# A mixture-of-experts pass whose first 256 tokens go through all experts as a dense layer, with smaller rooms for the rest and the weights loaded first

## The chip, the core and the metric

The kernel runs on one core of one Trainium2 chip. A core has TensorE (PE, matrix products; its weight loads are shown apart as PEld), VectorE (DVE), ScalarE (ACT), GpSimd (POOL) and SyncE (SP, which here only issues DMAs), and 16 DMA engines which all queues share. The metric is the device time of one execution in microseconds; given is the median of three runs.

## The reference, cut to what matters

The input is 8 sequences of 512 tokens with 128 features. Three residual steps follow each other: half a mixture-of-experts feed-forward, an attention with 16 heads of 8, and the same feed-forward again (same weights).

```python
def _L0_ffn_ref(x, router_w, router_b, W1, b1, W2, b2):     # 8 experts, 2 chosen, 128 -> 512 -> 128
    logits = jnp.einsum('bsd,de->bse', x, router_w) + router_b
    topk_scores, topk_idx = jax.lax.top_k(logits, TOP_K)
    topk_gates = jax.nn.softmax(topk_scores, axis=-1)
    onehot = jax.nn.one_hot(topk_idx, NUM_EXPERTS, dtype=x.dtype)
    combine = jnp.einsum('bsk,bske->bse', topk_gates, onehot)
...
    def expert_step(acc, params):
        w1, bb1, w2, bb2, c = params
        h = jax.nn.relu(jnp.einsum('bsd,df->bsf', x, w1) + bb1)
        y = jnp.einsum('bsf,fd->bsd', h, w2) + bb2
        return (acc + y * c[..., None], None)
...
x = L0_attn_x
x = x + 0.5 * _L0_ffn_ref(_layernorm(x, axis=-1), L0_ffn_router_w, ...)
x = x + _L0_attn_ref(_layernorm(x, axis=-1), L0_attn_w_qkv, L0_attn_w_o, L0_attn_log_xi)
x = x + 0.5 * _L0_ffn_ref(_layernorm(x, axis=-1), L0_ffn_router_w, ...)
```

Each token counts in only two of the eight experts. Everything is float32.

## The kernel before

**Tokens in rooms.** The kernel does not run every token through every expert. It forms six groups of sequences: f0 (sequences 0 and 1), f1 (2 to 4) and f2 (5 to 7) for the first feed-forward, g0, g1 and g2 for the second. `route` normalises a sequence, computes the router's logits on PE, ranks the experts on DVE, and counts with a few products by a triangle of ones (L844 to L852) which place in its expert's room each token gets. Eight indirect DMAs of POOL for each sequence (`scatter`, L875: four tiles of 128 tokens by two choices) then write the normalised rows into a buffer in memory, `xs`. A room is one expert's share of that buffer; for f0 it has 351 rows, for the others 480 (351 again for g0). Since a room is seldom full, `clear` (L700) first fills the buffer with zeros, which SP copies out of a tile of zeros.

**An expert's pass.** `experts` goes through a group's rooms. For each expert it fetches the room (L933), transposes it on PE (L976), ACT copies it out (L980), PE makes the four 128-wide slices of the hidden layer (`wide`, L989; called z), ACT applies bias and relu (L996), PE makes the outputs, one tile of up to 128 rows after the other (`out`, L1013; called y), DVE adds the bias (L1017), and SP writes the rows to a second buffer, `ys` (L1024). Products of one expert stand between those of the next in an order written out in `experts`. A fetch is issued about two experts ahead. `combine` gathers a token's two rows from `ys` by indirect DMAs of POOL (L474) and adds them, weighted, to `x` on DVE (L1073).

**What sets the order.** PE, ACT, DVE and SP keep the order in which the program records their instructions. POOL's transfers are entered in a list (`enter`) and taken from it by `transfer`. The program is a sequence of units, -30 to 125. The units from 0 to 95 each do one piece of attention; in all of them a plan (`plan`) says which group's expert pieces fill the unit: f0 from -30 to -16, f1 from -16 to 7, and so on. `at`, `routed` and `combined` put the routing, gathering and attention's projections at given units. Ahead of unit -30 stands a part that is written out by hand with `step` and `transfers`: the normalising of sequences 0 to 4 and the routing of 0, 1 and part of 2, with their scatters, so that f0 can be fetched.

**What SP loads, and when.** Ahead of the hand-written part SP issues, in this order, x of sequences 0 and 1, the clear of f0's buffer, x of 2, the weights and bias rows of experts 0 to 3 with x of 3 and 4 and the clear of f1's buffer between them, and small constants. The rest (`self.loads`: experts 4 to 7, x of 5 to 7, the attention weights, the clear of f2's buffer) is taken two at a time at the end of each unit from -30. All of SP's DMAs go through one queue, and each waits for the eighth before it.

**Pads.** Attention uses four tiles of 128 x 2048 (query, key, and two for values), which must be zero where no head writes. `slots` has ACT fill them at the start, 1.9 us each (L718). Small constants are written into them by `attention_constants` in unit -30.

**PSUM.** Up to unit 0 one pool of eight banks holds all products (`bank`).

## Time and profile before

| | us |
|---|---|
| median of 3 runs (715.65 to 717.79) | 716.47 |
| the profiled execution | 700.09 |
| its span on the core | 698.3 |
| PE busy | 629.2 (90%) |
| DVE busy | 410.2 (59%) |
| ACT busy | 341.3 (49%) |
| POOL busy | 300.3 (43%) |
| PE busy in the first 40 us of the span | 9.8 |
| f0's first transposes on PE | at 40.71 |
| f1's first transposes on PE | at 91.42 |

Sums and stages are read from the profiled execution, whose own time is 16 us under the median of the runs. Durations in the profile are from an instruction's start to its end; since products on PE overlap, what one of them costs is the distance between starts. In the rows by time, each digit is the busy share of one fortieth of the span (17.5 us) in tenths. Moved bytes: 61.06 MB over the span, 42.51 of them by SP's queue and 17.63 by POOL's indirect DMAs.

### The profile page before, as it was taken

The page shows a single profiled execution, that of the slowest core. Times are in us where ns is not written, and L with a number is a line of the kernel's source. Part 1 is how long each engine was busy: PE and PEld are TensorE (multiplying, and loading weights), DVE is VectorE, ACT ScalarE, POOL GpSimd, SP SyncE. Part 2 cuts the span into 40 slices and gives each one's busy share as a digit, 9 for nine tenths or more (in the row PEclk, how much of TensorE's full clock was granted, in tenths as well). Part 3 has the DMA queues.
Part 4 walks back from the last instruction along what each step waited for, and adds up shares of the span by engine and source line. Part 5 has one row for each costly group of instructions (what it writes and reads, how often), then busy time and mean ns, then how long its engine had stood idle before and what let it go on. Part 6 is the DMA issues. An engine that isn't in the chain of part 4 may idle for free. (4 is left out here: it accounts for less than half of the span.)

```text
span 698.3 us, 13045 instructions
## 1 busy us (share of the span) xinstructions
PE 629.2 (90%) x4867; PEld 410.3 (59%) x4867; DVE 410.2 (59%) x1442; ACT 341.3 (49%) x548; POOL 300.3 (43%) x322
## 2 busy tenths in 40 slices
PE   3269999999999999999999999999999998969980
PEld 2148867756465656556656656656456656747760
DVE  6736448734466666675687677676666654433414
ACT  4034443455755656565665565555665552234420
POOL 3744637642223223314154423424144556575660
PEclk9999999999999999999999999999999999889995
DMA  8747843312409921111211111101402111145324
GB/s 265 197 136 209 205 115 98 85 45 77 101 22 172 264 69 38 30 29 43 71 32 49 40 38 38 30 27 39 105 27 75 35 31 42 53 121 140 104 58 143
DMA packets 78670, 61.06 MB, mean 87 GB/s; under 512 B 7392, under 2 KB 70792, under 8 KB 78600
## 3 DMA queue, kind: packets, MB, share of 16 engines
q1 hardware_dynamic: 69608, 42.51, 23.8%
q0 software_dynamic: 8704, 17.63, 8.5%
q8 instruction: 41, 0.67, 0.4%
q14 instruction: 29, 0.24, 0.1%
q10 hardware_dynamic: 288, 0.01, 0.0%
HBM read 26.34 MB, written 33.78 MB: 86 GB/s over the span
## 5 line engine op out<-in xcount | busy, mean ns | idle before, releaser
L1208 ACT ACTIVATE ee<-st 128x768 f32<-128x768 f32 (+1 forms) x192 | 159.0, 881 | 104.1 <-PE st L1201 100.6
L474 POOL DMA_INDIRECT yt_f<-ys,back_f x64 | 64.8, 1013 | 133.5 <-DVE ee L1215 55.7
L1215 DVE TENSOR_TENSOR ee<-ee,keep 128x256 f32<-128x256 f32 (+1 forms) x192 | 93.5, 507 | 25.4 <-ACT ee L1208 25.3
L1013 PEld LDWEIGHTS y_g<-w_sb,h_g 128*120 128x120 f32 (+1 forms) x704 | 87.1, 184 | 27.4 <-issue 21.7
L875 POOL DMA_INDIRECT xs<-xn_g,to_g x64 | 63.8, 998 | 90.1 <-DVE ee L1215 34.9
L1013 PEld LDWEIGHTS y_f<-w_sb,h_f 128*120 128x120 f32 (+1 forms) x704 | 85.9, 182 | 28.5 <-issue 16.2
L1201 PE MATMUL st<-qT,kT 32*128 32x512 f32 (+3 forms) x1024 | 96.1, 467 | 2.3 <-ACT h_f L996 0.8
L1013 PE MATMUL y_f<-w_sb,h_f 128*120 128x128 f32 (+1 forms) x704 | 93.9, 277 | 0.2 <-DVE h_f L998 0.2
L989 PE MATMUL z_g<-xT_g,w_sb 128*128 128x480 f32 (+1 forms) x192 | 92.6, 569 | 1.3 <-ACT xT_g L980 1.3
L1013 PE MATMUL y_g<-w_sb,h_g 128*120 128x128 f32 (+1 forms) x704 | 93.0, 277 | 0.6 <-DVE o_tok L1250 0.3
L1227 PE MATMUL o<-ee,vpad 128*32 128x512 f32 (+3 forms) x1024 | 89.4, 442 | 0.8 <-DVE ee L1215 0.8
L989 PE MATMUL z_f<-xT_f,w_sb 128*128 128x480 f32 (+1 forms) x192 | 88.8, 551 | 1.0 <-ACT xT_f L980 1.0
L996 ACT ACTIVATE h_f<-z_f,b1T 128x480 f32<-128x480 f32 (+1 forms) x86 | 53.5, 623 | 68.2 <-PE z_f L989 67.3
L957 POOL DMA_INDIRECT ys<-ysb_g,home_g x64 | 63.7, 996 | 39.3 <-ACT h_g L996 8.7
L1017 DVE TENSOR_TENSOR ysb_f<-y_f,b_sb 120x128 f32<-120x128 f32 (+1 forms) x88 | 25.0, 287 | 77.9 <-PE y_f L1013 74.2
L996 ACT ACTIVATE h_g<-z_g,b1T 128x480 f32<-128x480 f32 (+1 forms) x71 | 45.7, 646 | 47.4 <-PE z_g L989 46.7
L1201 PEld LDWEIGHTS st<-qT,kT 32*128 32x128 f32 x1024 | 43.1, 183 | 32.6 <-issue 8.1
L1017 DVE TENSOR_TENSOR ysb_g<-y_g,b_sb 120x128 f32<-120x128 f32 (+1 forms) x88 | 25.1, 287 | 58.2 <-PE y_g L1013 57.6
L1227 PEld LDWEIGHTS o<-ee,vpad 128*32 128x32 f32 x1024 | 23.5, 108 | 52.4 <-issue 7.5
L875 POOL DMA_INDIRECT xs<-xn_n,to_f x40 | 39.0, 974 | 34.9 <-ACT xi_sb L727 8.1
L989 PEld LDWEIGHTS z_g<-xT_g,w_sb 128*128 128x128 f32 x192 | 30.1, 195 | 26.6 <-issue 15.2
L989 PEld LDWEIGHTS z_f<-xT_f,w_sb 128*128 128x128 f32 x192 | 30.2, 194 | 13.8 <-issue 7.2
(186 smaller groups left out, 778.7 us busy)
## 6 DMA issues: line engine op xcount, KB each, us to landing
w_sb<-in_L_ffn_W_dram SPq DMA_DIRECT2D x16, 256.0 KB
xs<-zeros SPq DMA_DIRECT2D x8, 487.5 KB
xb_g<-xs SPq DMA_DIRECT2D x16, 243.8 KB
xb_f<-xs SPq DMA_DIRECT2D x16, 240.0 KB
ys<-ysb_f SPq DMA_DIRECT2D x16, 240.0 KB
ys<-zeros SPq DMA_DIRECT2D x2, 1536.0 KB
x<-in_L_attn_x_dram SPq DMA_DIRECT2D x8, 256.0 KB
xs<-zeros SPq DMA_DIRECT2D x1, 1920.0 KB
```

What stands on the lines that cost most here:

```text
L474: ins = op(*args, **kw)
L875: ins = nc.gpsimd.indirect_dma_start(out=g.xs[:, :], out_offset=bass.IndirectOffsetOnAxis(ap=g.to[:, i, t, r : r + 1], axis=0), in_=xn[:, ...
L957: ins = nc.gpsimd.indirect_dma_start(out=g.ys[:, :], out_offset=bass.IndirectOffsetOnAxis(ap=home[e][:rows, t : t + 1], axis=0), in_=ys[:r ...
L989: nc.tensor.matmul(z[:, :n], self.w1_sb[:, e, ts(c, P)], xT[:, n0 : n0 + n], start=True, stop=True,)
L996: ins = nc.scalar.activation(dst, z[:, :n], AF.Relu, bias=bias)
L1013: nc.tensor.matmul(y[:rows], h[:, c, ts(t, rows)], self.w2_sb[:, e, c, :], start=(c == 0), stop=(c == C - 1),)
L1017: ins = nc.vector.tensor_tensor(ys[:rows, t, :], y[:rows], self.b2_sb[:rows, e], ALU.add)
L1201: nc.tensor.matmul(st[:, h, c0 : c0 + N - kt * P], kT[r0 : r0 + SLOT, ts(kt, P)], qT[r0 : r0 + SLOT, kt * P :], start=True, stop=True,)
L1208: nc.scalar.activation(ee[:, two, :width], st[:, two, :width], AF.Exp)
L1215: ins = self.nc.vector.tensor_tensor(d, d, self.keep.unsqueeze(1).unsqueeze(1).to_broadcast([P, 2, len(parts), P]), ALU.min,)
L1227: self.nc.tensor.matmul(self.o[h * SLOT : (h + 1) * SLOT, kt * P :], self.vpads[b % 2][:, kt, 4 * g + h, :], ee[:, h, c0 : c0 + n], start= ...
```

## The change

It has four parts.

1. **A dense layer.** The first 256 tokens of sequence 0 (`f0.skip[0] = 2`, two tiles of 128) are no longer scattered, fetched and gathered. A new function, `dense`, runs them through all eight experts straight from the transposed rows which the router uses as well, and adds each expert's output to x with the token's gate for that expert (`shares`, zero for the six that were not chosen). Its pieces stand between the steps of the hand-written part.
2. **Smaller rooms.** f0 has 252 rows for each expert, in two tiles of 126, instead of 351 in three of 117; its buffer is cleared in pieces of 1 KB. It has 12 scatters instead of 16, and sequence 0 four gathers instead of eight. g0 keeps 351 rows.
3. **Weights first.** All eight experts' weights are issued ahead of the hand-written part, with the clear of f0's buffer after the first, and x of 2 to 4 and the clear of f1's buffer further back. The bias rows of the second product, spread over the partitions, and the attention constants are loaded from the list from unit -30 on. The column biases (`bias_columns`) are prepared at the very start.
4. **Blanks by DMA.** The four pads are filled by SP's queue from the tile of zeros (`blank`), in the same list, instead of by ACT. `attention_constants` moves from unit -30 to -14.

The core of the diff:

```diff
-ROOMS = [(2, 351, False), (3, 480, False), (3, 480, False), (3, 480, True), (3, 480, True)]
+ROOMS = [(2, 252, False), (3, 480, False), (3, 480, False), (3, 480, True), (3, 480, True)]
...
-        self.clear(0)
-        self.load_x(2)
         self.w1_sb = const.tile([P, E, FF], FP, name="w1_sb")
         self.w2_sb = const.tile([P, E, C, D], FP, name="w2_sb")
         self.b2_sb = const.tile([P, E, D], FP, name="b2_sb")
+        b1_sb = load("b1_sb", [E * C, P], aps["b1"].rearrange("e (c p) -> (e c) p", p=P), nc.scalar)
+        self.b2_rows = load("b2_rows", [E, D], aps["b2"], nc.scalar)
+        for e in range(E):
+            self.load_expert(e)
+            if e == 0:
+                self.clear(0)
+            if e == 3:
+                self.load_x(2)
+        self.load_x(3, 4)
+        self.clear(1)
         self.slots()
-        b1_sb = load("b1_sb", [E * C, P], aps["b1"].rearrange("e (c p) -> (e c) p", p=P))
-        for e in range(4):
-            self.load_expert(e, True)
-            self.load_expert(e, False)
-            if e == 0:
-                self.load_x(3, 4)
-            if e == 2:
-                self.clear(1)
-        self.rope_sb = load("rope_sb", [P, 2, T, DH], aps["rope"])
-        pos_sb = load("pos_sb", [P, T], aps["pos"])
-        xi_sb = load("xi_sb", [P, H], aps["log_xi"].partition_broadcast(P))
+        self.rope_sb = const.tile([P, 2, T, DH], FP, name="rope_sb")
+        pos_sb = const.tile([P, T], FP, name="pos_sb")
+        xi_sb = const.tile([P, H], FP, name="xi_sb")
         self.wqkv_sb = const.tile([P, 3 * D], FP, name="wqkv_sb")
         self.wo_sb = const.tile([P, D], FP, name="wo_sb")
-        self.loads = deque(partial(self.load_expert, e, up) for e in range(4, E) for up in (True, False))
-        self.loads.insert(3, partial(self.load_x, 5))
-        self.loads.insert(6, partial(self.load_x, 6))
+        self.loads = deque(
+            partial(nc.sync.dma_start, dst, src) for dst, src in (
+                *((self.b2_sb[:, e], aps["b2"][e].partition_broadcast(P)) for e in range(E)),
+                (self.rope_sb, aps["rope"]), (pos_sb, aps["pos"]),
+                (xi_sb, aps["log_xi"].partition_broadcast(P)),
+            )
+        )
+        self.loads.append(partial(self.load_x, 5))
+        self.loads.extend(partial(self.blank, pad) for pad in (self.qpad, self.kpad, *self.vpads))
         self.loads.extend([
-            partial(nc.sync.dma_start, self.wqkv_sb, aps["w_qkv"]), partial(self.load_x, 7),
-            partial(nc.sync.dma_start, self.wo_sb, aps["w_o"]),
+            partial(self.load_x, 6), partial(nc.sync.dma_start, self.wqkv_sb, aps["w_qkv"]),
+            partial(self.load_x, 7), partial(nc.sync.dma_start, self.wo_sb, aps["w_o"]),
         ])
         self.loads.extend(partial(self.clear, 2, t) for t in range(4))
...
-    def load_expert(self, e, up):
+    def load_expert(self, e):
         nc, aps = self.nc, self.aps
-        if up:
-            nc.sync.dma_start(self.w1_sb[:, e, :], aps["w1"][e])
-        else:
-            nc.sync.dma_start(self.w2_sb[:, e], aps["w2"][e].rearrange("(c p) d -> p c d", p=P))
-            nc.sync.dma_start(self.b2_sb[:, e], aps["b2"][e].partition_broadcast(P))
+        nc.sync.dma_start(self.w1_sb[:, e, :], aps["w1"][e])
+        nc.sync.dma_start(self.w2_sb[:, e], aps["w2"][e].rearrange("(c p) d -> p c d", p=P))
+
+    def blank(self, pad):
+
+        flat = pad.rearrange("p t h s -> p (t h s)")
+        self.nc.sync.dma_start(
+            flat.rearrange("p (a d) -> p a d", d=T * D),
+            self.zeros[:, : T * D].unsqueeze(1).to_broadcast([P, flat.shape[1] // (T * D), T * D]),
+        )
 
...
-        for t_ in (self.qpad, self.kpad, *self.vpads):
-            self.nc.scalar.copy(
-                t_.rearrange("p t h s -> p (t h s)"),
-                self.zeros[:, 0:1].to_broadcast([P, T * H * SLOT]),
-            )
-
...
+        if g.skip[i]:
+            self.dense_xT = xnT
...
         pp = self.bank([P, 512], f"pos_ps_{key}")
         pos = pp[:, : T * E].rearrange("p (t e) -> p t e", e=E)
-        nc.tensor.matmul(pos, self.earlier, mask, start=True, stop=False)
-        for t in range(T - 1):
+        nc.tensor.matmul(pos[:, t0:], self.earlier, mask[:, t0:], start=True, stop=False)
+        for t in range(t0, T - 1):
             nc.tensor.matmul(
...
-        self.enter([partial(scatter, t, r) for t in range(T) for r in range(2)], urgent, ahead)
+        self.enter(
+            [partial(scatter, t, r) for t in range(t0, T) for r in range(2)], urgent, ahead
+        )
...
+        if t0:
+            shares = small.tile([P, t0, E], FP, tag="shares", name=f"shares_{key}")
+            nc.vector.scalar_tensor_tensor(
+                shares, rank[:, :t0], 2.0, ex[:, :t0], ALU.is_lt, ALU.mult
+            )
...
+        if t0:
+            nc.vector.tensor_tensor(
+                shares, shares, g.gates[:, i, :t0, 0:1].to_broadcast([P, t0, E]), ALU.mult
+            )
+            self.shares = shares
...
+    def dense(self, b, nt):
+
+        nc = self.nc
+        n = nt * P
+        x = self.x[b]
+        h = {}
+
+        def up(e):
+            h[e] = self.fp.tile([P, C, CAP], FP, tag="h", name=f"h_d_{e}")
+            for k in range(0, C, 2):
+                z = self.bank([P, 2, n], f"z_d_{e}_{k}")
+                for j in range(2):
+                    nc.tensor.matmul(
+                        z[:, j], self.w1_sb[:, e, ts(k + j, P)], self.dense_xT[:, :n],
+                        start=True, stop=True,
+                    )
+                for j in range(2):
+                    c = k + j
+                    nc.scalar.activation(
+                        h[e][:, c, :n], z[:, j], AF.Relu, bias=self.b1T[:, e * C + c : e * C + c + 1]
+                    )
+
+        def down(e):
+            y = self.bank([P, nt, D], f"y_d_{e}")
+            for t in range(nt):
+                for c in range(C):
+                    nc.tensor.matmul(
+                        y[:, t], h[e][:, c, ts(t, P)], self.w2_sb[:, e, c, :],
+                        start=(c == 0), stop=(c == C - 1),
+                    )
+
+            def add():
+                for t in range(nt):
+                    nc.vector.scalar_tensor_tensor(
+                        x[:, t, :], y[:, t], self.shares[:, t, e : e + 1], x[:, t, :],
+                        ALU.mult, ALU.add,
+                    )
+
+            return add
+
+        up(0)
+        yield
+        adds = []
+        for e in range(E):
+            if e + 1 < E:
+                up(e + 1)
+                yield
+            adds.append(down(e))
+            while len(adds) > 2:
+                adds.pop(0)()
+            yield
+        for add in adds:
+            add()
+
+        tp = self.bank([P, 512], "shT_ps")
+        for t in range(nt):
+            nc.tensor.transpose(tp[:E, ts(t, P)], self.shares[:, t, :], self.ident)
+        sT = self.const.tile([E, n], FP, name="shT")
+        nc.scalar.copy(sT, tp[:E, :n])
+        yield
+        bp = self.bank([P, nt, D], "b2_ps")
+        for t in range(nt):
+            nc.tensor.matmul(bp[:, t], sT[:, ts(t, P)], self.b2_rows, start=True, stop=True)
+        nc.vector.tensor_tensor(x[:, :nt], bp, x[:, :nt], ALU.add)
+        yield
...
-        self.enter([partial(gather, t, r) for t in range(T) for r in range(2)], urgent, ahead)
+        self.enter(
+            [partial(gather, t, r) for t in range(g.skip[i], T) for r in range(2)], urgent, ahead
+        )
...
-        f0 = m.open_group([0, 1], 351, 0, "f0")
+        f0 = m.open_group([0, 1], 252, 0, "f0")
+        f0.skip[0] = 2
...
-            r = [m.route(f0, 0, early=True), m.route(f0, 1, early=True), m.route(f1, 0, True, early=True)]
+            r = [
+                m.route(f0, 0, early=True), m.route(f0, 1, early=True),
+                m.route(f1, 0, True, early=True),
+            ]
+            d = m.dense(0, f0.skip[0])
+            m.bias_columns()
             step(n[0], n[0], n[1], n[1], n[0], n[0])
-            step(r[0], n[1], n[1], r[0], r[1], r[0], r[0])
+            step(r[0], n[1], n[1], r[0], d, r[1], r[0], d, r[0])
+            transfers(4)
+            step(d, r[0], r[1], d, r[0], r[1], d, r[0], r[1], n[2], n[2])
             transfers(8)
-            step(r[1], r[1], r[1], n[2], n[2])
+            step(d, d, n[2], n[2], d, r[2], d, r[1], d, r[2], d, r[1], d, r[2], r[1], d)
+            step(n[3], n[3], n[4], n[4], r[2], d)
             transfers(8)
-            step(n[3], n[3], n[4], n[4], *[r[0], r[1]] * 3, n[2], n[2])
-            step(r[2], r[2], r[2], n[3], n[4], n[3], n[4])
-            run(*r[:2], *n)
-            m.bias_columns()
-
-            at(first, r[2], 4)
+            step(d, d, n[3], n[3], n[4], n[4])
+            run(d, *r[:2], *n)
+
+            at(first, r[2], 3)
...
-                if u == first:
+                if u == -14:
                     m.attention_constants()
```

## The prediction

> **What bounds the kernel now.** I read the page's rows by time first, to see where TensorE (PE) is not full; then the table of stretches; then PE's waits; then the timeline at the places found.
>
> ```profile
> PE 629.2 (90%) x4867; PEld 410.3 (59%) x4867; DVE 410.2 (59%) x1442; ACT 341.3 (49%) x548; POOL 300.3 (43%) x322
> ...
> PE   3269999999999999999999999999999998969980
> ...
> DMA  8747843312409921111211111101402111145324
> ```
> PE is full but for the first two slices and the tail. What moves PE's start of full work, and adds or removes PE work after it, moves the end nearly one for one.
>
> ```profile
> 30.00:40.00 10.00, 1.33 (x7) 1.15 (x7) 4.67 (x17) 0.00 (x0) 7.14 (x8) 1.00 0.24 75
> ...
> PE xbT_ps_f L976 <- DMA xb_f<-xs: 10.2, 2, 9.4
> ...
> 35.68 0.96 POOL L875 DMA_INDIRECT xs<-xn_n,to_f  x1 [0.30 <-issue]
> ...
> 37.93 1.79 SPq L933 DMA_DIRECT2D xb_f<-xs  x4
> ...
> 40.71 0.82 PE L976 MATMUL xbT_ps_f<-ident,xb_f 117*128 117x117 f32 x3 [9.38 <-DMA xb_f<-xs]
> ```
> The columns of the first line are busy us of PE, weight load, DVE, ACT and POOL, then clock, DMA share and GB/s. Up to 40.71 PE works some 10 us; it waits 9.4 us for the first group's rows. Before that POOL issues f0's 16 scatters back to back, one per 1.27 us, from 15.4 to 36.6. From 40.71 to 90.6 PE runs group f0 without a gap, and at 91.42 starts f1.
>
> ```profile
> 9.00 1.88 PE L814 MATMUL lg_ps_f<-rw_sb,xnT_f 128*128 128x8 f32 x8 [0.78 <-DVE xnT_f L786]
> ...
> 50.59 0.96 PE L814 MATMUL lg_ps_f<-rw_sb,xnT_f 128*128 128x8 f32 x8
> ...
> 52.95 0.76 PE L989 MATMUL z_f<-xT_f,w_sb 128*128 128x351 f32 x2
> ...
> 53.54 1.04 PE L1013 MATMUL y_f<-w_sb,h_f 128*117 128x128 f32 x8
> 54.42 0.76 PE L989 MATMUL z_f<-xT_f,w_sb 128*128 128x351 f32 x2
> ```
> Starts, not durations, give PE's price: an up product (z) of 351 columns holds PE 53.54-52.95 = 0.59 us, a down tile (y) 54.42-53.54 = 0.88. That is 1.7 ns a column and product. The same logits cost 1.88 us at 9.0 and 0.96 at 50.6.
>
> ```profile
> 69.18 0.89 SPq L700 DMA_DIRECT2D xs<-zeros  x1
> ...
> 71.54 6.30 SPq L700 DMA_DIRECT2D xs<-zeros  x3
> ...
> 88.38 1.18 SPq L933 DMA_DIRECT2D xb_f<-xs  x2
> ...
> 91.42 0.60 PE L976 MATMUL xbT_ps_f<-ident,xb_f 120*128 120x120 f32 x4 [0.84 <-DMA xb_f<-xs]
> ...
> 75.00:80.00 5.00, 5.00 (x35) 4.21 (x34) 2.46 (x15) 2.56 (x5) 3.48 (x5) 1.00 0.95 234
> ```
> During f0 SP's queue is already backed up (three clears took SP 6.3 us, DMA share 0.95), but it is empty again (share 0.38 in 85 to 90) when f1's rows are fetched; they come 3 us after the issue and PE waits 0.84.
>
> **What the Trainium skill says.** (1) "TensorE: Matmul & The Clock Gate", What's actually happening: PE runs at half rate until about 3.4 us of sustained work, and falls back after an idle window. The trace agrees: 1.88 against 0.96 us above, and z pairs come down to 0.6 us some 3 to 4 us after 40.71. (2) "DMA: Bandwidth & Descriptors", Queues, rings and completion order: one queue's descriptors are consumed in ring order on the 16 engines, so a fetch stands behind bulk copies issued before it by SP. The 6.3 us above agree. (3) Same page, Where 436 GB/s comes from: SBUF-to-SBUF copies are held by the fabric at 435 GB/s. No run here has such a copy.
>
> **The change, part by part.** The time sums are on the profiled span (698.3 us; that execution was 700.1; the median of the runs is 716.5, and I carry the difference over).
>
> *Start.* b1T is now DVE's first work after the memsets, ahead of the layer norm that began at 4.01. Its load is third on ACT's queue (0.45 us each, so issued near 1.7), lands near 4, then transpose and copy: +0.7 us on all that follows. Blanking the four pads (4 x 1.9 us of ACT) goes off ACT, where nothing waited.
>
> *Dense layer.* Per expert four z of 256 columns at 0.44 and two y at 0.88: 3.5 us, 28.0 for eight. Logits of sequence 0 start at 9.7. PE is then cold for about 4.4 us (40.7 to 45 in the trace): logits 1.8, z of expert 0 at double price 3.5, to 15.0. Warm from there: transposes of sequence 1 0.45, z of expert 1 1.75, to 17.2. The mask of sequence 0 comes 1.2 late (copy 0.69 and four DVE steps of 0.42 behind those transposes); position matmuls, to 18.7. The rest runs on: eight y pairs 14.0, six z 10.5, two logits 1.75, transposes 0.45, positions 0.3 = 27.0, to 45.7. Sequence 2's normalised rows are 0.3 late (positions, statistics, power on POOL, 5.5 us against 5.25 of PE work). Transposing the shares, ACT's copy and the bias product: 1.6. Sum 47.6: f0 can start at 48 instead of 40.7. In the built program the y matmuls wait for ACT's relus alone; the banks that DVE's late additions hold are not taken again at once, so those waits cost nothing. ACT needs 4 x 0.47 = 1.9 of each 3.5 us. DVE's 16 additions (0.36) and the extra routing steps lie under PE's work.
>
> *Weights first.* Bytes ahead of expert 1: x, w0, clear 0, w1, 2.3 MB, at 310 GB/s by about 10 us; wanted at 15. The others follow every 2 us, wanted every 3.5 to 6: hidden. All of SP's first 8.5 MB have landed by about 32; x2 by 15.
>
> *Scatters.* 12 instead of 16. Sequence 1's eight start behind POOL's power for sequence 2, at 29, end at 40; rows land as before 4 us later, 44: before 48, hidden, but close.
>
> *f0 in rooms of 252.* Per expert: transposes 0.22 (was 0.30), four z of 0.43 (0.60), two y tiles instead of three: 3.7 us instead of 5.3. Eight: 29.5 instead of 42.6. With starting latency 0.9 and the routing inside it 4.5 (three transposes and logits, two positions) f0 takes 34.9 and ends at 82.9 instead of 90.6. So PE alone would gain 7.7 us.
>
> *The pads and what stands behind them.* This is the disputed term. Four blanks of 1 MB now go through SP's queue in 2 KB pieces. In SP's built order they stand behind the third result of f0 (y of expert 2: 16.7 us into f0, at 64.7), and before the fetch of f1's rows stand: pads 4.2 MB, the query weights 0.2, two x 0.5, the output weights 0.07, f0's last fetch 0.13, four results 0.5, clear 2 2.0, then f1's first rows 0.25: 7.85 MB. Eleven scatters add 0.7. Low bound, packets at their uncontended price (2 KB 84 ns, 512 B 27 ns on one of 16 engines): 25 us. At the rates of saturated stretches here (310 GB/s for large pieces, 255 for 512 B): 30. I take 28, plus 1.5 to the semaphore: f1's rows are in at 94.2. If these copies run at half rate it is 38 us, at the fabric's price nearer 23. PE would be ready at 83: it waits 11 us, and f1 starts at 94.2 instead of 91.4: +2.8. f0's own last rows, behind the first two pads, land near 72.5 and are wanted at 74: hidden, barely. PE has then gone cold and pays about half of 3.4 us again: +1.7.
>
> *After that.* The additions and gathers of sequence 0 halve: four gathers less (1.27 us of POOL each), hidden under f1; PE's wait of 0.9 us for the first queries (at 136.8) may go: -0.5. f1, attention and the second feed-forward are the same instructions.
>
> Sum: 2.8 + 1.7 - 0.5 = +4.0: span 702.3, that execution 704.1, median 720.5.
>
> **The rivals.** *A, faster: the queue drains in time.* If the bytes behind expert 2's result need under 17 us, f1 starts when PE is done, at 83.7: -7.7 -0.5, 708.3. For it: before, a similar heap of clears was gone by 84 and PE never saw it. Against: that heap was about 4.2 MB in 19 us; now it is 8.5 MB in 18. The turning point for any gain is about 23 us (f1 at 89.7, cold restart paid). *B, slower still: SBUF-to-SBUF copies at half rate* (38 us): f1 at 104, +14, 730. Nothing in the trace prices them. *C, the dense layer is late*: if PE stays at half rate longer, or the small stalls turn it cold again, or the positions hold the next product, f0 starts at 53 to 54. All after it moves by 5 to 6, the pads too: about 726. Against it: PE has under 1.5 us of waits in a row there. That the scatters hold f0 (44 against 48) would show only if PE were faster than reckoned.
>
> **How the numbers follow.** A measurement of this kernel can't tell less than about 0.3%, 2.1 us, from no change. My forecast (queue decides, -1 to +9) has 0.53, A with all between -9 and -1 has 0.25, B 0.1, C 0.12. Slower by over 2.1: 0.38 of my case, B and C: 0.60. Same: 0.16 from mine and 0.03 of A: 0.19. Faster: 0.21. The likeliest case's own range is 715 to 726; the range reaches to A's and C's times at 709 and 729, and leaves out half of B.
>
> **What would show it.** Right: a start of f0's first transposes near 48; PE near full from 15 on; z pairs of 252 at 0.43; SP's blanks issued near 65 with a DMA share near 1 for 25 us; and PE's longest wait at f1's first transposes, for the fetch of its rows, about 11 us. Wrong: that wait under 3 us (A), the blanks' packets above 150 ns (B), or f0 starting after 52 with PE waits for DVE or weights in the dense layer (C).

## The result, and the profile after

The changed kernel takes 727.88 us (median, 727.05 to 729.62) beside 716.09 for the kernel before in the same comparison: ratio 1.0163, 95% interval 1.0137 to 1.019, so 11.8 us slower where 4.0 were forecast. On one occasion every run of the kernel before takes near 701 us and on another near 716, even on the same chip some 35 minutes apart, so each time below stands beside that of the kernel before on the same occasion, and profiles of two kernels are set side by side only where the kernel before took the same. The execution of the kernel before that the prediction read (700.09) was of the first kind, the profiled execution after (729.62, span 727.6) of the second.

The page of the changed kernel, its rows by engine and by time:

```profile
PE 657.3 (90%) x4991; PEld 434.3 (60%) x4991; DVE 412.2 (57%) x1449; ACT 342.1 (47%) x577; POOL 294.9 (41%) x314
...
PE   4989669989999999999999999999999987978980
...
DMA  8723972322224971011301111111412111244324
```

The first two slices are fuller than before (4 and 9, where the kernel before has 3 and 2): the dense layer fills the hole in which PE had waited for f0's rows. In its place stands a new hole in slices 5 and 6 (6, 6; from 73 to 109 us), just where the DMA row has 9 and 7.

PE's waits of the first 200 us, the costliest first (us in total, times, longest):

```profile
PE xbT_ps_f L999 <- DMA xb_f<-xs: 6.7, 1, 6.7
PE b_ps L679 <- DMA b_sb<-in_L_ffn_b_dram: 6.1, 1, 6.1
PE y_f L1036 <- ACT h_f L1019: 4.9, 2, 2.5
```

The timeline of PE (start, us, what, and in brackets the idle time before it):

```profile
11.45 1.88 PE L822 MATMUL lg_ps_f<-rw_sb,xnT_f 128*128 128x8 f32 x8 [0.78 <-DVE xnT_f L792]
13.18 3.76 PE L1099 MATMUL z_d<-xnT_f,w_sb 128*128 128x256 f32 x8
...
51.27 0.44 PE L999 MATMUL xbT_ps_f<-ident,xb_f 126*128 126x126 f32 x2
...
82.49 0.48 PE L1036 MATMUL y_f<-w_sb,h_f 128*126 128x128 f32 x2 [2.40 <-ACT h_f L1019]
...
89.91 0.49 PE L1036 MATMUL y_f<-w_sb,h_f 128*126 128x128 f32 x2 [2.50 <-ACT h_f L1019]
...
104.02 1.03 PE L999 MATMUL xbT_ps_f<-ident,xb_f 120*128 120x120 f32 x4 [6.69 <-DMA xb_f<-xs]
```

And SP's queue:

```profile
70.93 0.70 SPq L694 DMA_DIRECT2D qpad<-zeros  x1
71.68 0.64 SPq L694 DMA_DIRECT2D kpad<-zeros  x1
...
76.37 3.13 SPq L694 DMA_DIRECT2D vpad<-zeros  x2
...
98.24 2.65 SPq L956 DMA_DIRECT2D xb_f<-xs  x2
```

The forecast's picture is there: the pads go out during f0, the fetch of f1's first rows stands behind them (98.24, 27 us after the first pad), and PE's longest wait in this part is for those rows. But the logits start at 11.45 instead of 9.7, f0 at 51.3 instead of 48, and f1 at 104.0 instead of 94.2. And f0 itself, forecast at 34.9 us, takes 46.1 (from 51.27 to 97.33, where the wait for f1's rows begins); the two waits of 2.4 and 2.5 us for ACT's relus lie within it.

### The profile page after: what moved, and what is told of

Same layout as the page of the kernel before. It is cut to its first block, busy times and chain, and to the rows that moved or that the text cites. A ratio compares the mean times of both kernels' runs of the same rounds, so it can differ in the third digit from the quotient of the medians.

```text
span 727.6 us, 13327 instructions
## 1 busy us (share of the span) xinstructions
PE 657.3 (90%) x4991; PEld 434.3 (60%) x4991; DVE 412.2 (57%) x1449; ACT 342.1 (47%) x577; POOL 294.9 (41%) x314
## 4 chain that ended last, share of the span: by engine, by line
PE 66%; DVE 4%; issue 3%; DMA 2%; ACT 1%; POOL 1%; another core or an unknown queue 0%; POOLq 0%; SPq 0%; ACTq 0%
PE st L1292 12%; PE o L1318 11%; PE z_g L1012 10%; PE y_g L1036 9%; PE y_f L1036 6%; PE z_f L1012 5%; PE qkv_ps_a L1230 3%; PE kT_ps L1269 2%; PE otok_ps L1336 2%; PE qT_ps L1269 2%; PE xbT_ps_g L999 1%; DVE x L1205 1%; PE proj_ps L1357 1%; PE lg_ps_g L822 1%; POOL ys L980 1%
## 5 line engine op out<-in xcount | busy, mean ns | idle before, releaser
L475 POOL DMA_INDIRECT yt_f<-ys,back_f x60 | 61.1, 1018 | 145.1 <-DVE ee L1306 53.6
L1036 PEld LDWEIGHTS y_g<-w_sb,h_g 128*120 128x120 f32 (+1 forms) x704 | 88.6, 186 | 32.8 <-issue 24.3
L1036 PE MATMUL y_g<-w_sb,h_g 128*120 128x128 f32 (+1 forms) x704 | 94.9, 280 | 5.4 <-ACT h_g L1019 2.5
L1036 PEld LDWEIGHTS y_f<-w_sb,h_f 128*120 128x120 f32 (+1 forms) x640 | 79.4, 186 | 30.3 <-issue 16.2
L1036 PE MATMUL y_f<-w_sb,h_f 128*120 128x128 f32 (+1 forms) x640 | 87.5, 280 | 5.1 <-ACT h_f L1019 4.9
L1012 PE MATMUL z_f<-xT_f,w_sb 128*128 128x480 f32 (+1 forms) x192 | 86.7, 544 | 1.9 <-ACT xT_f L1003 1.4
L1019 ACT ACTIVATE h_f<-z_f,b1T 128x480 f32<-128x480 f32 (+1 forms) x86 | 50.4, 594 | 73.7 <-PE z_f L1012 44.4
L1040 DVE TENSOR_TENSOR ysb_f<-y_f,b_sb 120x128 f32<-120x128 f32 (+1 forms) x80 | 22.7, 287 | 75.9 <-PE y_f L1036 58.5
L1292 PEld LDWEIGHTS st<-qT,kT 32*128 32x128 f32 x1024 | 43.1, 183 | 34.3 <-issue 8.2
L886 POOL DMA_INDIRECT xs<-xn_n,to_f x36 | 35.7, 991 | 33.3 <-DVE to_f L875 11.1
L1012 PEld LDWEIGHTS z_f<-xT_f,w_sb 128*128 128x128 f32 x192 | 31.9, 202 | 16.6 <-issue 9.7
```

What stands on the lines that cost most here:

```text
L475: ins = op(*args, **kw)
L886: ins = nc.gpsimd.indirect_dma_start(out=g.xs[:, :], out_offset=bass.IndirectOffsetOnAxis(ap=g.to[:, i, t, r : r + 1], axis=0), in_=xn[:, ...
L1012: nc.tensor.matmul(z[:, :n], self.w1_sb[:, e, ts(c, P)], xT[:, n0 : n0 + n], start=True, stop=True,)
L1019: ins = nc.scalar.activation(dst, z[:, :n], AF.Relu, bias=bias)
L1036: nc.tensor.matmul(y[:rows], h[:, c, ts(t, rows)], self.w2_sb[:, e, c, :], start=(c == 0), stop=(c == C - 1),)
L1040: ins = nc.vector.tensor_tensor(ys[:rows, t, :], y[:rows], self.b2_sb[:rows, e], ALU.add)
```

## The experiments

In every fence below a PE line has its start, its length and, in brackets, the wait before it.

**The two kernels on the first kind of occasion (e1, e5).** Neither is edited.

> The kernel before, unchanged. Its first profile stands 16 us under the median of its runs. If that execution was a lucky one, this profile has a span of 712 to 716 us, and the difference to the first profile sits in waits of DVE, ACT and PE that no semaphore explains (none longer than 0.7 us in the first profile, 27 us each on DVE and ACT in the profile of the changed kernel). If such waits are the changed kernel's own, the span is near 699 again and they are absent. Ratio to before 1.000 in both.

> The changed kernel, unchanged, beside the kernel before on the chip of the first four experiments, where the kernel before takes 701.75. Theory Q (f1's rows stand behind the pads in SP's queue; the column biases delay the start): e2, with the pads on ACT, took 699.6, e3, with the biases later, 707.8, so both costs together give 709 to 711, ratio 1.010 to 1.013; f0's first transposes near 50, PE's longest wait at f1's first transposes, and no waits of ACT and DVE that nothing explains beyond what the kernel before shows. Rival W (the waits of ACT and DVE that nothing explains, some 27 us on each in the first profile of the changed kernel, come with the change): they appear again, over 15 us on each, and the time is 715 or more.

e1: 701.44, ratio 1.000 (0.9987 to 1.0013), span 699.5. e5: 709.0 beside 701.45, ratio 1.0099 (1.0061 to 1.0137), so +7.5 us; span 705.7. That is the lower edge of theory Q's range. e1's span is the one that its second reading expected, but what decides between 699 and 712 is the occasion and not the kernel, as e13 shows below. PE's timeline of e5, and of e1:

```profile
49.15 0.43 PE L999 MATMUL xbT_ps_f<-ident,xb_f 126*128 126x126 f32 x2
...
99.06 1.03 PE L999 MATMUL xbT_ps_f<-ident,xb_f 120*128 120x120 f32 x4 [12.30 <-DMA xb_f<-xs]
```

```profile
41.18 0.82 PE L976 MATMUL xbT_ps_f<-ident,xb_f 117*128 117x117 f32 x3 [9.84 <-DMA xb_f<-xs]
...
92.37 0.60 PE L976 MATMUL xbT_ps_f<-ident,xb_f 120*128 120x120 f32 x4 [0.77 <-DMA xb_f<-xs]
```

This is the pair in which the forecast's steps can be checked: f0 8.0 us later, f1 6.7 us later, PE's wait 12.3 us. The times that the expectations of e2, e3 and e4 give were reckoned from the first comparison's 728 us; what can be checked is their distance from the changed kernel, e5. Setting the two sequences of products side by side, the changed kernel is 8.4 us late at the first product of attention, still 8.4 at 570, and 6.0 at 632.

**The pads on ACT again (e2), or on SP's queue but later (e7).**

```diff
 e2:
-        self.loads.extend(partial(self.blank, pad) for pad in (self.qpad, self.kpad, *self.vpads))
...
+        for t_ in (self.qpad, self.kpad, *self.vpads):
+            self.nc.scalar.copy(t_.rearrange("p t h s -> p (t h s)"), ...)
 e7 (the four blanks are taken out of the list and kept in m.blanks):
+                if u >= -16 and m.blanks:
+                    m.blanks.popleft()()
-                if u == -14:
+                if u == -12:
                     m.attention_constants()
```

> The changed kernel with one part undone: ACT fills the four pads at the start, as before; SP's queue loses 4.2 MB. Theory A, that f1's rows wait behind those copies: PE's 6.7 us wait at f1's first transposes goes and with it most of the half-rate restart after it (about 4 us), so 716 to 719 us against 728. Theory B, that the stretch of f0 is long because of the waits of ACT and DVE that no semaphore explains, independent of the queue: the two ACT waits near 80 and 87 us stay, and no more than 3 us are gained, 725 to 728. Theory C, that PE's added products are simply not hidden: no change, 728.

> The changed kernel with the four blanks still copied by SP's queue, but one in each of the units -16 to -13 instead of -25 to -23, so behind the fetches of f1's first rooms; the attention constants move from unit -14 to -12. Theory Q (what costs is the place in the queue, ahead of f1's first rows): 698 to 702, about e2, and PE's wait at f1's first transposes falls from some 10 us to under 3. Rival C (the copies cost wherever they stand, since they hold the DMA engines for 16 us and delay what is fetched meanwhile): 706 to 710, with the wait moved to f1's second to fourth rooms or to the first queries of attention.

e2: 699.63, ratio 0.9963 (0.9947 to 0.9979): against e5 it is 0.0136 less, 9.5 us (theory A expected 9 to 12), and a little faster than the kernel before. e7: 701.89, ratio 0.9995 (0.9979 to 1.0011). In e7 the same 4.2 MB go through the same queue, only behind the fetches of f1's first rooms; f1 then starts at 89.38 and PE waits 1.63 us for its rows. SP's queue in e5 and in e7, and PE in e7:

```profile
66.49 0.70 SPq L694 DMA_DIRECT2D qpad<-zeros  x1
...
93.86 2.21 SPq L956 DMA_DIRECT2D xb_f<-xs  x2
```

```profile
86.29 1.16 SPq L956 DMA_DIRECT2D xb_f<-xs  x2
...
89.63 0.69 SPq L694 DMA_DIRECT2D qpad<-zeros  x1
```

```profile
89.38 0.60 PE L999 MATMUL xbT_ps_f<-ident,xb_f 120*128 120x120 f32 x4 [1.63 <-DMA xb_f<-xs]
```

So 7.3 of the 9.5 us (e7 against e5) are the pads' place in the queue, and not the copies as such (rival C of these runs). The other 2.3 (e7 against e2, with intervals that touch) can be the copies' own: in e7's profile PE later waits 1.2 us for normalised rows, at 120.4, which e2's does not show.

**That part of the change alone, on the kernel before (e8).** Edit: the function `blank` and its four entries in SP's list behind the weights of expert 7, ACT's four copies taken out, the attention constants in unit -14.

> The kernel before with this part of the change alone: the pads filled by SP's queue, after the weights of the eighth expert in its list, and the attention constants in unit -14. Theory Q: f0 lasts 50 us here, against about 35 to 40 in the changed kernel, so the 8.5 MB that are then issued during f0 drain in about 33 us and f1's rows come in at 91 to 95, where PE asks for them at 91.4: 701 to 706, ratio 1.000 to 1.006. Rival C (the copies cost wherever they stand): 8 to 10 us, 710 to 712, ratio 1.012 or more.

711.72, ratio 1.0138 (1.0094 to 1.0182): +10.3 us. The number is the rival's, but the place of the wait is theory Q's, in PE's timeline of e8:

```profile
101.00 1.04 PE L979 MATMUL xbT_ps_f<-ident,xb_f 120*128 120x120 f32 x4 [9.65 <-DMA xb_f<-xs]
```

The pads are issued at 66.7, f1's rows are in at 101.0: 34.3 us. My expectation that a longer f0 would hide the heap failed: in the kernel before, f1's rows already came 0.8 us late, so its queue had no room for 4 MB more. What f1's start follows is the pads' issue, wherever that stands: f1 starts 32.6 us after it in e5, 32.6 and 32.8 in e3 and e4 below (where it comes 2.1 and 7.7 us earlier than in e5), and 33.1 in the profile after.

**The start: column biases later (e3), and both repairs together (e6).**

```diff
-            m.bias_columns()
             step(n[0], n[0], n[1], n[1], n[0], n[0])
+            m.bias_columns()
```

> The changed kernel with the column biases transposed and copied after the normalising of sequence 0 instead of before it. DVE then starts at 4.0 us instead of 6.5. If PE sets the end from the start on, 2.5 us less, 725.4; if the pads' copies set f1's start, the same, since they are issued by f0's progress; if the first weights or something else hold PE at the start, no gain, 728.

> The changed kernel with the pads on ACT again (as in e2) and with the column biases prepared after sequence 0 is normalised (as in e3). If the two costs are independent: e2's 699.6 less what e3 gains over the changed kernel of this run (1 to 3 us), so 696.5 to 698.5, ratio 0.993 to 0.996, f0's first transposes near 46. Rival: with the pads on ACT the biases are not what is late at the start (ACT is busy with the pads for 7.6 us and hands over the transposed rows late anyway): 699 to 700, the same as e2.

e3: 707.8, ratio 1.0081 (1.0051 to 1.0111); f0 starts at 47.1 instead of 49.15, f1 at 97.0 instead of 99.1, and PE still waits 12.3 us there. The time is 1.3 us under e5, with overlapping intervals, where 2.5 were expected. e6: 696.37, ratio 0.9918 (0.989 to 0.9947), 3.2 us under e2, just below the range of independent costs, with f0 at 47.4 instead of 46. So the biases at the start cost 1 to 3 us, and on this occasion the dense layer, the smaller rooms and the earlier weights are worth some 5 us once the pads are off the queue and the biases out of the way.

**The dense layer's products left out (e4), and f0's rooms of 351 rows again (e11).** e4 omits the layer's products, its relus and its additions; e11 is e2 with the two sizes 252 put back to 351.

> The changed kernel without the dense layer's products, relus and additions (so the first 256 tokens get no expert's output but the second biases); its transposed shares and all the rest stay. Theory A with the forecast's sum: f0 can start when its scatters are in, near 43 instead of 51.3, and everything after it moves by about 8: 719 to 721. Theory C, that the 28 us of PE work are fully on the path: 700. If the scatters or the pads alone decide: 726 to 728.

> The kernel of e2 (pads on ACT) with f0's rooms of 351 rows again, in three tiles of 117; the dense layer and the skipped scatters stay. By the prices of the prediction an expert of f0 costs 1.6 us more, f0 13 us more. Theory P (PE's own time then sets f1's start, and the wait of 3.3 us goes): f1 starts near 101 instead of 90.8, less 1.7 for a restart that isn't cold: 707 to 709. Rival: DVE's and ACT's work or the scatters set f0's pace: under 704.

e4: 700.99, ratio 0.9994, 7.4 us under e5 by the ratios: theory A's 8, and not the 28 of theory C. f0 then starts at 39.7, 9.5 us before e5, and f1 at 91.7, 7.4 before it, with the same wait of 12.6 us in between: the queue carries the gain of f0's start to f1, but not the wait. e11: 709.21, ratio 1.0089 (1.0058 to 1.012), so the smaller rooms are worth 8.9 us. PE's timeline of e11 has f1 at 99.34 where e2 has 90.83:

```profile
99.34 0.93 PE L1004 MATMUL xbT_ps_f<-ident,xb_f 120*128 120x120 f32 x4 [2.25 <-DMA xb_f<-xs]
```

I had asked for 13 us on PE. It is 8.7 (f0 lasts 48.1 us here, 39.4 in e2), and the wait does not go (2.25 us): the larger rooms' own time is as reckoned (42.6 + 0.9 + 4.5 = 48.0), and it is the smaller ones that take more than 34.9.

**What holds f1's rows when the pads are gone (e9), and whether the queue or the engines held them (e10).** In e9, from e6, the routing of sequences 3 and 4 enters at units -30 and -29 instead of -29 and -27. In e10, from the changed kernel:

```diff
-            nc.sync.dma_start(
+            eng = nc.gpsimd if key == "f1" and e < 3 else nc.sync
+            eng.dma_start(
                 xb[:rows, : g.ct, : g.width],
```

> The kernel of e6 (pads on ACT, column biases after sequence 0) with the routing of sequences 3 and 4 entered at units -30 and -29 instead of -29 and -27. In e6 PE is done with f0 at 85.0 and waits 4.3 us; the last of f1's scatters is issued at 82.0, SP's fetch follows at 86.3, the rows at 89.3. Theory S (once the pads are out of the queue, f1's scatters on POOL decide): the last scatter comes 2 to 4 us earlier, f1 starts at 85.5 to 87.5 and PE pays less or nothing for being cold: 692 to 694.5. Rival Q (the clears of f2's buffer in SP's queue still decide): the fetch does not move, 695.5 to 697.5.

> The changed kernel, pads still in SP's queue at the same place, with the fetches of f1's first three rooms issued by POOL right behind its last scatter, in POOL's own queue. Theory Q (the order in SP's queue decides): these rows pass the heap; the last scatter is issued at 84.8 in e5, so rows come some 8 us later, f1 starts at 92 to 95 instead of 99.1, PE's wait falls from 12.3 to 5 to 8, time 702 to 705. Rival E (what decides is that the DMA engines are full up to 98, whatever the queue): f1 starts at 97 or later, 707 to 710.

e9: 695.8, ratio 0.9901 (0.9876 to 0.9926), not to be told from e6; f1 starts at 88.48. Theory S's 692 to 694.5 and its f1 before 87.5 did not come. The waits of SP's own queue (what SP waits for before it issues the fetch, us in total, times, longest) between 60 and 100, first of e6:

```profile
SPq L961 <- DMA xs<-xn_n,to_f: 3.6, 1, 3.6
```

and of e9:

```profile
SPq L961 <- DMA xs<-xn_n,to_f: 2.5, 1, 2.5
```

With the pads gone SP is ready to fetch and waits for the last of f1's 24 scatters to land. In e6 the last one is issued at 82.0, the fetch at 86.3, the rows come at 89.3; PE was done at 85.0. In e9 the last scatter goes out 2.3 us earlier and the fetch only 0.9, since the fetch follows that scatter's issue by 5.7 us instead of 4.2. The DMA share is 0.94 to 0.98 from 78 to 82 in both, while f2's buffer is cleared; that the clears slow the landing is a reading, not shown.

e10 is split. In its profiled execution (702.81) theory Q's numbers come: the rows issued by POOL pass SP's heap, and PE has them at 92.77,

```profile
92.77 1.03 PE L1000 MATMUL xbT_ps_f<-ident,xb_f 120*128 120x120 f32 x4 [6.69 <-DMA xb_f<-xs]
```

although the DMA share is 0.95 or more from 76 to 90, so full engines alone do not hold a fetch in this execution. This agrees with what the Trainium skill says in "DMA: Bandwidth & Descriptors", Queues, rings and completion order: on each DMA engine it is the descriptors of one ring, which belongs to one queue, that are taken in order. But the other three executions took 708 to 711.6 (median of all four 708.31, ratio 1.0103, 1.0073 to 1.0134), the rival's number, and none of them was profiled. Where those 6 us lie stays open.

**The second kind of occasion (e12 to e18).** e12 is e9 with f2's four clears issued behind f1's, ahead of the hand-written part.

> The kernel of e9 with the four clears of f2's buffer (2 MB) issued ahead of the hand-written part, right behind the clear of f1's buffer, instead of during f0. In e9 the last of f1's scatters is issued at 79.7, but SP's fetch waits for it to land until 85.4, while the DMA share is 0.96 from 78 to 82. Theory L (the clears keep the engines full and so delay the scatters' landing): the scatters land by 82, the fetch goes out behind the result before it at 82.8, rows at 85.8 to 86.5, PE waits 1 to 1.5 us instead of 3.3 and is less cold: 692 to 694. Rival: the scatters' latency behind POOL is what it is; f1 stays at 88, 695 to 697. What could go wrong: the clears, in the queue at 32 to 40, delay the scatters or the fetch of f0, then f0 starts at 49 or later and the time is 698 or more.

> The kernel before, unchanged, for a profile beside the next three in one call. If the waits of ACT and DVE that nothing explains belong to the occasion and not to a kernel, then either all four profiles of this call have them (the kernel before near 716, its profile with over 15 us of such waits on ACT and on DVE) or none has (near 701).

> The changed kernel, unchanged. With the kernel before near 701: 708 to 710 (ratio 1.010), as in e5. With it near 716: 726 to 729 (ratio 1.014 to 1.018), as in the first comparison; the share above 7.5 us then lies where such waits stretch the dense layer and f0, so that f0 starts after 51 and f1 after 103. Rival: the first comparison's 11.8 us was chance, and the ratio is 1.010 on either occasion.

> The kernel of e12 (pads on ACT, column biases later, routing of sequences 3 and 4 a unit earlier, f2's clears ahead of the hand-written part). With the kernel before near 701: theory L, 692 to 695 (ratio 0.986 to 0.991); the rival of e12 (the clears are then in the way of f0's start), 699 or more. With it near 716: again about the same as the kernel before.

> The kernel of e9, without the early clears of e12. With the kernel before near 701: 695 to 697 (ratio 0.990), as in e9. With it near 716: 712 to 716 (ratio 0.995 to 1.000); if it is under 0.993 there too, e12's tie comes from its early clears and not from the occasion.

> The kernel of e12 and e15 once more, to have it on an occasion where the kernel before takes near 701 (there e9, without the early clears, took 695.8, ratio 0.990). If this is such an occasion: theory L, 691 to 694 (ratio 0.985 to 0.989), f1's first transposes at 85.5 to 87 with a wait under 2 us; its rival (no gain from the early clears) 695 to 697. If the kernel before takes near 716: 0.998 to 1.002 as in e12 and e15.

> The kernel of e9 and e16 beside it in the same call. With the kernel before near 701: 695 to 697 (ratio 0.990); near 716: 716 to 719 (ratio 1.001 to 1.005). Theory L: e17 is 2 to 4 us faster than this run on either occasion.

All seven fell where the kernel before takes 716:

| run | kernel | median, us | ratio to before, with interval |
|---|---|---|---|
| e13 | before | 715.62 | 1.0009 (0.9988 to 1.003) |
| e14 | changed | 724.85 | 1.015 (1.0104 to 1.0196) |
| e12 | early routes and clears | 715.23 | 1.0003 (0.9982 to 1.0024) |
| e15 | the same | 715.01 | 0.9998 (0.9974 to 1.0022) |
| e17 | the same | 719.2 | 1.0026 (1.0005 to 1.0047) |
| e16 | early routes | 717.92 | 1.0032 (1.0012 to 1.0052) |
| e18 | the same | 720.83 | 1.0073 (1.0038 to 1.0109) |

The change is 1.5% to 1.6% slower here (e14 and the first comparison), 1.0% on the other kind; and the repaired kernel, 1% faster there, is 0.3% to 0.7% slower here. The early clears gain 1.6 us (e17 against e18) to 2.9 (e15 against e16), in the direction expected, with overlapping intervals; in the profiles of e12, e15 and e17 SP does not wait for f1's scatters at all, but for f0's results, so theory L itself is not tested. No kernel tried is faster than the kernel before on this kind of occasion; the early clears were never measured on the other.

Much of what the changed kernels lose here, they lose in f0. In the kernel before f0, up to where the wait for f1's rows begins, takes the same on both kinds of occasion (50.4 us in e1, 49.9 in e13). With rooms of 252 it takes 37.6 and 38.1 on the first kind (e5, e9) and 43.9 to 48.5 on the second (the profile after, e12, e14, e15, e17, e18). The stretch of f0 in e5 and in the profile after (length, busy us of PE, weight load, DVE, ACT and POOL, then clock, DMA share and GB/s):

```profile
49.15:86.76 37.61, 35.83 (x256) 31.86 (x255) 21.84 (x90) 16.73 (x43) 21.42 (x22) 1.00 0.70 217
```

```profile
51.27:97.33 46.06, 39.76 (x256) 34.58 (x255) 23.59 (x98) 16.75 (x43) 23.14 (x24) 0.93 0.69 209
```

PE's waits inside it grow from 1.8 to 6.3 us, most of it for ACT's relus, and its granted clock there falls from 1.00 to 0.93. So the kernel of e9, whose f1 starts 3.9 us before that of the kernel before on the first kind (88.48 and 92.37), is 3.1 us behind it on the second (97.23 in e18, 94.09 in e13):

```profile
88.48 1.03 PE L1004 MATMUL xbT_ps_f<-ident,xb_f 120*128 120x120 f32 x4 [3.32 <-DMA xb_f<-xs]
```

```profile
97.23 0.60 PE L1004 MATMUL xbT_ps_f<-ident,xb_f 120*128 120x120 f32 x4 [0.99 <-DMA xb_f<-xs]
```

e14's ratio is the expected one, but its f0 (49.74) and f1 (102.45) start before the expected 51 and 103; e16 and e17 are slower than expected.

I had counted as a mark of this occasion the waits of ACT and DVE that the profile gives to nothing ("issue", "remote"). That count is no measure. The same DVE instruction, first in e13 and then in e1:

```profile
267.27 0.29 DVE L1017 TENSOR_TENSOR ysb_f<-y_f,b_sb 120x128 f32<-120x128 f32 x1 [2.08 <-issue]
```

```profile
261.41 0.29 DVE L1017 TENSOR_TENSOR ysb_f<-y_f,b_sb 120x128 f32<-120x128 f32 x1 [2.09 <-PE y_f L1013]
```

The wait is the same, only its name has gone. What counts is where PE falls behind. Side by side with e1, e13 is less than 0.6 us late up to 92, 5.8 by 127 (f1's rows come 1.7 us later and find PE cold), 7 to 8 by 610, and 13.0 at 632. There PE waits for ACT's copy of the transposed rows; in e13 and then in e1:

```profile
632.41 1.97 PE L989 MATMUL z_g<-xT_g,w_sb 128*128 128x480 f32 x2 [5.92 <-ACT xT_g L980]
```

```profile
619.39 1.97 PE L989 MATMUL z_g<-xT_g,w_sb 128*128 128x480 f32 x2 [0.65 <-ACT xT_g L980]
```

ACT's own idle time before that copy is 15.2 us, put down to nothing, against 9.5 for the transposes in e1. e14 beside e5 loses in other places, 2.35 us of PE in one step of f0 and 3.4 at 598 among them:

```profile
80.57 0.48 PE L1036 MATMUL y_f<-w_sb,h_f 128*126 128x128 f32 x2 [2.35 <-issue]
```

ACT stands just before it, 3.71 us up to 80.05, where the profile names nothing; between the same products of e5 it never stands longer than 0.84. Why ACT stands, and why only on some occasions, stays open.

## Why the prediction was right and wrong, step by step

Measured on e5 and e1, whose occasion is that of the profile it was made from.

- **Direction and mechanism: right.** "The pads and what stands behind them" is what makes the change slower. Taking the pads out of the way gives back 9.5 us (e2) with the rest of the change in place, and 7.3 of them come back when the pads only move behind f1's first fetches (e7).
- **Start: direction right, size off.** The step had the biases' load "lands near 4" and +0.7 us. It landed at 6.18 in e5 (6.08 in the profile after), DVE's statistics began at 6.61 instead of 4.01, and the logits started at 11.55 instead of 9.7: 1.85 late.
- **Dense layer: right.** From the logits to f0's first transposes 37.9 us were reckoned (9.7 to 47.6); it took 37.6. f0 began at 49.15 instead of 48. Rival C did not happen on this occasion; f0 at 51.3 in the first profile comes near it.
- **f0 in rooms of 252: short by 2.7 us.** 34.9 reckoned, 37.6 measured (49.15 to 86.76). PE's time by kind: z 14.6 (13.8 reckoned), y 14.6 (14.1), transposes 2.0 (1.8), routing 4.6 (4.5), waits 1.8 (0.9): a little in every term, the most in waits and z. That is the first kind of occasion; in the profile after f0 took 46.1, with 6.3 us of waits. The forecast has no wait inside f0 but 0.9 of starting latency; there ACT's relus held the products.
- **"PE alone would gain 7.7 us": not to be had.** This is the step that was wrong in kind, and with it rival A's 708.3; the sum itself does not use it. The working checked f0's scatters against f0's start but not f1's scatters against f1's start. POOL issues the last of them at 82.0 to 84.6 in e2, e5 and e6 (79.7 in e9), and the fetch waits for them: without the pads f1 starts at 88.5 to 90.8 (e2, e6, e9), never near 83.7. PE itself is done with f0 at 85.0 in e6 and at 87.6 in e2. Two shorter stages in front of a chain of scatters do not shorten the chain.
- **Queue behind the pads: the step that failed, the term of the sum that was mis-sized most.** The issue was forecast at 64.7, it came at 66.5 (f0's later start and its slower pace: 17.3 us into f0 instead of 16.7). From there 29.5 us were reckoned to the rows, 32.6 came. The rate was nearly right: 8.55 MB in 28 us would be 305 GB/s, and the stretch in e5 ran at 296:

```profile
66.50:99.06 32.56, 18.95 (x132) 16.49 (x130) 11.48 (x51) 8.34 (x21) 14.43 (x15) 0.86 0.99 296
```

  (length, the five engines' busy us, clock, DMA share, GB/s). 32.56 us at 296 GB/s are 9.6 MB: a megabyte more than listed. By queue it is 8.6 MB of SP's (7.85 listed: parts of f1's next fetches move with the first, and there is one more result) and 1.0 of scatters (0.7). f1's start 99.06 - 92.37 = +6.7 instead of +2.8. In the profile after the same steps miss by more: f0 starts 3.3 us later than forecast, the pads go out 19.7 us into f0 instead of 16.7, and from there 33.1 us pass instead of 29.5. That makes f1's 104.0 instead of 94.2, 9.9 us behind e13.
- **PE's wait "about 11 us": right,** 12.3. So was full rate for the pads (rival B): their 2 KB packets take 88 ns at the median in e5, against the 84 of the forecast, and the stretch from 70 to 80 moved 354 GB/s. The Trainium skill, "DMA: Bandwidth & Descriptors", Where 436 GB/s comes from, gives 435 GB/s as the limit of copies inside SBUF; this stretch, which mixes them with other transfers, stays under it, and no run here tests it.
- **Cold restart +1.7: right at its place, short in all.** Beside e1, e5 is 6.7 us late at f1's first transposes and 8.6 late 5 us further on: +1.9. Another 0.7 joins it by 130 us, at the transposes of normalised rows, for which the forecast has no term: 9.3 late, +2.6.
- **"After that", -0.5: right as far as it went.** PE's wait for the first queries was to go at half its size; it went whole, and e5 falls from 9.3 to 8.4 us late there. PE in e1 and in e5:

```profile
137.76 0.63 PE L1178 MATMUL qT_ps<-ident,qpad 128*128 128x128 f32 x4 [0.88 <-DVE qpad L1165]
```

```profile
146.19 0.63 PE L1269 MATMUL qT_ps<-ident,qpad 128*128 128x128 f32 x4
```

  e8, which saves no gathers, keeps a wait of 0.97 us there, as the forecast's reason asks. A further 2.4 us come back between 593 and 618 of e1, which no term foresaw. Most of that isn't the saved gathers: e8 gets 1.7 back there (12.4 late at attention, 10.7 at 638).
- **The sum.** Forecast 2.8 + 1.7 - 0.5 = +4.0; with the measured terms 6.7 + 2.6 - 0.9 - 2.4 = +6.0, and the two spans differ by 6.2, the medians by 7.5. So two misses in part cancel: the queue's term was 3.9 us too small, and 2.4 us that nobody had counted came back. The other 2 to 4 us of the first comparison belong to its occasion (e14 gives +9.2 there), where f0 is longer. Carrying a sum made on one execution over to the median of another kind of occasion was itself a step, and it wasn't free.

## What to carry to other kernels

Work that leaves an idle engine for a DMA queue isn't free: find the next transfer that PE waits for in that queue, add up all the bytes between, with the indirect transfers and the pieces of later fetches, and either issue the bulk behind that transfer or leave it where it was. Before a stage is shortened, follow every chain that must end with it, here a run of scatters at 1.27 us each; a gain on one engine stops at the next such chain. Test a gain of one per cent on more than one occasion.

## What the runs showed of the hardware that I had not expected

- One chip gave 701.75 us for the kernel before and, some 35 minutes later, 716.24; two further chips gave 715.6 to 715.8, two others 701.45 and 702.24. Beside e1, e13 loses 5.3 us of PE in one wait for ACT, and for ACT's own wait the profile names nothing.
- Executions of one kernel differ by up to 6 us, along with their granted clock: e2, whose profile has a gap of 3.3 us ahead of f1, gave 695.5 to 697 in the four executions with a clock of 0.977, and 698.5 to 701.9 in the eleven with 0.970 to 0.973. That PE's clock falls after that gap in some executions and not in others would explain it; that is argued only.
- The fetch that waited for the last scatter of 128 rows went out 4.2 us after that scatter's issue in e6 and 5.7 in e9, with DMA shares of 0.94 to 0.98 from 78 to 82 in both.
